# Recommender forward pass: a fill of 224 columns behind every gather, tables split by TensorE, transposes tile by tile with drifting token rows

## Chip, cores, metric

One core of a Trainium2 chip. The metric is the time of one execution in microseconds of that core. The runs of this study fell on several chips of the same kind. They are named by their numbers, because the chip also belong here: on chips 1, 11, 13 and 14 the kernel before takes about 5265 us, on chips 5 and 7 and in the measurement that the prediction is held against about 7120 us. Below, the first are called **quick chips**, the second **slow chips**. Ratios are the mean time of one kernel's fast runs over that of the other's of the same rounds on the same chip, so they are not quite the ratio of the medians quoted beside them.

## The reference

16,384 examples. Each has 32 token ids (table of 50,000 x 300), three lists of 20 ids (tables of 1,000, 5,000 and 10,000 rows of 64) and four single ids.

```python
tok = word_emb[token_idx].mean(axis=1)
e1 = emb_mh1[mh1_idx].mean(axis=1)      # e2, e3 alike
o1 = emb_oh1[oh1_idx]                   # o2, o3, o4 alike
emb = jnp.concatenate([tok, e1, e2, e3, o1, o2, o3, o4], axis=1)     # 748 wide
wide = (wide_mh1[mh1_idx].sum(axis=(1, 2)) + ...)[:, None]           # one number each
h = jax.nn.relu(emb @ W1 + b1)          # 748 -> 1024
h = jax.nn.relu(h @ W2 + b2)            # -> 512
h = jax.nn.relu(h @ W3 + b3)            # -> 256
return jax.nn.sigmoid(h @ Wd + bd + wide)
```

## The kernel before

Examples are worked on in 128 tiles of 128. The token rows come by 32 gathers per tile, 4096 in all, issued by GpSimd and added up by VectorE in pairs:

```python
for q in range(n_groups):                     # 16 pairs per tile
    rows = tokp.tile([P, TOK_GROUP * TOK_D], F32, name="tok_rows")     # 6 buffers
    for r in range(TOK_GROUP):
        j = q * TOK_GROUP + r
        nc.gpsimd.indirect_dma_start(                                  # L224
            out=rows[:, r * TOK_D : (r + 1) * TOK_D], out_offset=None, in_=word,
            in_offset=bass.IndirectOffsetOnAxis(ap=it[:, j : j + 1], axis=0))
    under_way.append((t, q, rows))
    if len(under_way) > TOK_LAG:
        add_up(*under_way.pop(0))             # VectorE, L211 to L215
```

The small tables are not gathered: VectorE makes one-hot rows, TensorE multiplies them into counts, ScalarE evicts the counts and TensorE multiplies them with the tables. A tile has 11 such steps, 1408 in all:

```python
pc = ps_c.tile([P, 2, 2, 512], F32, name="pc")        # one buffer
... nc.tensor.matmul(pc[...], hot[0][half, k, :], hot[1][half, k, :])  # L312, 12 per step
nc.scalar.activation(cnt[...], pc[...], AF.Copy, scale=0.5)            # L319, 1.5 us
... nc.tensor.matmul(pg[:, j, :], by_slice[:, :, h], terms[:, h, :])   # L337, 138 per tile
```

The layers run on blocks of four tiles, in matmuls of 512 columns spread over the steps:

```python
x = xp.tile([P, NK, BLOCK], F32, name="x", tag="even")     # BLOCK = 512
yield from transposed(x, gs)              # four tiles at once, six chunks
yield from layer(h1, w1_sb, b1_sb, x, chunk_k, M1, n)      # matmul L388, eviction on ScalarE
...
sizes = [NSUB] * (tiles // NSUB - 1) + [NSUB - 2, 1, 1]    # last blocks: 2, 1 and 1 tiles
```

Each f32 table is split into three bf16 terms by ScalarE and VectorE at the start (`scalar_tensor_tensor`).

Of the kernel before, what the change touches and what calls it, by code (L numbers as in the profile page):

```python
# [23 lines left out]
TOK_LAG = 3  # L24
BLOCK = 512
HALF = P // 2
N_SMALL = 3 * N_MH + 4
ONEHOT = 6
STEPS = -(-HALF // ONEHOT)
CHUNK_WORK = 1  # L30
TABLE_PACE = 1.2
LAYER_TIME = 10
# [6 lines left out]
G_COLS = TOK_D + 7 * ROW  # L39
# [7 lines left out]
def kernel(  # L47
# [23 lines left out]
    NSUB = BLOCK // P  # L71
# [5 lines left out]
    for f in SMALL:  # L77
# [4 lines left out]
    tokp = ctx.enter_context(tc.tile_pool(name="tok", bufs=2 * TOK_LAG))  # L82
    const = ctx.enter_context(tc.tile_pool(name="const", bufs=1))
    idxp = ctx.enter_context(tc.tile_pool(name="idx", bufs=2))
# [4 lines left out]
    gp = ctx.enter_context(tc.tile_pool(name="g", bufs=NSUB + 1))  # L89
    wp = ctx.enter_context(tc.tile_pool(name="wide", bufs=2 * NSUB))  # L90
    xp = ctx.enter_context(tc.tile_pool(name="x", bufs=1))
# [8 lines left out]
        [(0, 128)],  # L100
        [(128, 256)],
        [(256, 300), (684, 748)],
        [(300, 428)],
        [(428, 556)],
        [(556, 684)],
    ]
# [7 lines left out]
    scale = const.tile([P, NK], F32, name="scale")  # L114
    nc.vector.memset(scale, 1.0)
    nc.vector.memset(scale[:, 0:2], 1.0 / N_TOK)
    nc.vector.memset(scale[0 : TOK_D - 256, 2:3], 1.0 / N_TOK)
    nc.vector.memset(scale[:, 3:4], 1.0 / N_MH)
    nc.vector.memset(scale[0:EMB, 4:5], 1.0 / N_MH)
# [23 lines left out]
    PART = n_h // 6  # L143

    def load_tables(part0, tag):
        raw = xp.tile([P, PART, ROW], F32, name="raw", tag=tag)
        for f in SMALL:
            table, (h0, h1) = tables[f], slices[f]
            full, rest = divmod(table.shape[0], P)
            a, b = max(h0, part0), min(h0 + full, part0 + PART)  # L150
            if a < b:
                nc.sync.dma_start(
                    out=raw[:, a - part0 : b - part0, :],
                    in_=table[(a - h0) * P : (b - h0) * P, :].rearrange("(h p) d -> p h d", p=P),
                )
            if rest and part0 <= h0 + full < part0 + PART:
                nc.vector.memset(raw[:, h0 + full - part0, :], 0.0)
                nc.sync.dma_start(out=raw[0:rest, h0 + full - part0, :], in_=table[full * P :, :])
        return raw

    def convert_tables():


        tags = ("even", "odd")
        raws = [load_tables(k * PART, tags[k]) for k in range(2)]
        yield
        for part in range(n_h // PART):
            rows = raws[part]
            if 1 <= part < n_h // PART - 1:
                raws.append(load_tables((part + 1) * PART, tags[(part + 1) % 2]))  # L170
            for c in range(3):
                term = [
                    terms[:, part * PART : (part + 1) * PART, k * ROW : (k + 1) * ROW]
                    for k in range(3)
                ]
                if c:
                    nc.vector.scalar_tensor_tensor(
                        rows, rows, 2.0 if c == 1 else 1.0, term[c - 1], op0=ALU.mult, op1=ALU.subtract
                    )
                nc.scalar.activation(term[c], rows, AF.Copy, scale=2.0 if c == 0 else 1.0)  # L180
                yield 1
# [20 lines left out]

    n_groups = N_TOK // TOK_GROUP
    under_way = []
    features = {}

    def add_up(t, q, rows):
# [4 lines left out]
        else:  # L212
            nc.vector.tensor_add(tok_sum, tok_sum, a)  # L213
            to = features[t][:, 0:TOK_D] if q == n_groups - 1 else tok_sum
            nc.vector.tensor_add(to, tok_sum, b)  # L215

    def tokens(t, it):


        for q in range(n_groups):  # L220
            rows = tokp.tile([P, TOK_GROUP * TOK_D], F32, name="tok_rows")
            for r in range(TOK_GROUP):
                j = q * TOK_GROUP + r
                nc.gpsimd.indirect_dma_start(  # L224
                    out=rows[:, r * TOK_D : (r + 1) * TOK_D],
                    out_offset=None,
                    in_=word,
                    in_offset=bass.IndirectOffsetOnAxis(ap=it[:, j : j + 1], axis=0),
                )
            under_way.append((t, q, rows))  # L230
            if len(under_way) > TOK_LAG:
                add_up(*under_way.pop(0))
            yield 1

    def last_tokens():
        for group in under_way:
            add_up(*group)

    def load_indices(blk):
# [15 lines left out]
        return it, ix  # L255
# [71 lines left out]
    def small_sums(g, cnt):  # L327
# [3 lines left out]
        for i in (0, 2, 4, 6):  # L331
# [9 lines left out]
            at = TOK_D + i * ROW  # L341
# [9 lines left out]
    def wide_term(g):  # L351
        wide = wp.tile([P, 1], F32, name="wide")
        at = TOK_D + EMB
        nc.vector.tensor_reduce(
            wide,
            g[:, at : at + 6 * ROW].rearrange("p (c d) -> p c d", d=2 * ROW)[:, :, 0:2],
# [3 lines left out]
        nc.vector.tensor_add(wide, wide, g[:, G_COLS - 1 : G_COLS])  # L360
        return wide

    def chunk(g, k):
        if k < 2:
            return g[:, k * P : (k + 1) * P]
        if k == 2:
            return g[:, 2 * P : TOK_D + EMB]
        at = TOK_D + (1 + 2 * (k - 3)) * ROW + 1
        return g[:, at : at + 2 * EMB]

    def transposed(x, gs):

        n = len(gs) * P
        for k in range(NK):
            kk = chunk_k[k]
            pt = ps_h.tile([P, BLOCK], F32, name="pt", tag="ph")
            for s, g in enumerate(gs):
                nc.tensor.transpose(pt[:kk, s * P : (s + 1) * P], chunk(g, k), ident)  # L378
            nc.vector.tensor_scalar(  # L379
                x[:kk, k, 0:n], pt[:kk, 0:n], scale[:kk, k : k + 1], None, ALU.mult  # L380
            )
            yield CHUNK_WORK

    def layer(dst, weights, bias, src, kks, n_out, n):
        for m in range(n_out):
            ph = ps_h.tile([P, BLOCK], F32, name="ph", tag="ph")
            for k, kk in enumerate(kks):
                nc.tensor.matmul(  # L388
                    ph[:, 0:n],
                    weights[:kk, k, m * P : (m + 1) * P],  # L390
                    src[:kk, k, 0:n],
                    start=(k == 0),
                    stop=(k == len(kks) - 1),
                )
                if k < len(kks) - 1:
                    yield 1
            nc.scalar.activation(dst[:, m, 0:n], ph[:, 0:n], AF.Relu, bias=bias[:, m : m + 1])  # L397
            yield 1

    def mlp(b0, gs, wides):  # L400

        n = len(wides) * P
        x = xp.tile([P, NK, BLOCK], F32, name="x", tag="even")
        yield from transposed(x, gs)
        h1 = xp.tile([P, M1, BLOCK], F32, name="h1", tag="odd")
        yield from layer(h1, w1_sb, b1_sb, x, chunk_k, M1, n)
        h2 = xp.tile([P, M2, BLOCK], F32, name="h2", tag="even")
        yield from layer(h2, w2_sb, b2_sb, h1, [P] * M1, M2, n)
        h3 = xp.tile([P, M3 + 1, BLOCK], F32, name="h3", tag="odd")
        yield from layer(h3, w3_sb, b3_sb, h2, [P] * M2, M3, n)  # L410
        po = ps_h.tile([1, BLOCK], F32, name="po", tag="ph")
        for k in range(M3):
            nc.tensor.matmul(  # L413
                po[:, 0:n], wd_sb[:, k : k + 1], h3[:, k, 0:n], start=(k == 0), stop=False
            )
        for s, wide in enumerate(wides):
            nc.tensor.matmul(  # L417
                po[:, s * P : (s + 1) * P], wide, ident, start=False, stop=(s == len(wides) - 1)
            )
        y = h3[0:1, M3, 0:n]  # L420
        nc.scalar.activation(y, po[:, 0:n], AF.Sigmoid, bias=bd_sb)
# [3 lines left out]
    class Paced:  # L425


        def __init__(self, gen):
            self.gen, self.done = gen, 0

        def to(self, size):
            while self.done < size:
                work = next(self.gen, None)
                if work is None:
                    return
                self.done += work
# [27 lines left out]

    tiles = B // P
    mlp_time = (NK * (CHUNK_WORK + M1) + M1 * M2 + M2 * M3 + M3) * LAYER_TIME
    ctx.enter_context(tc.manual_schedule())
    sizes = [NSUB] * (tiles // NSUB - 1) + [NSUB - 2, 1, 1]
    it, ix = load_indices(0)
# [5 lines left out]
    gs, wides, layers, before, b0 = [], [], None, None, 0  # L475
    for t in range(tiles + 1):
        s = t % NSUB
        sums = None
        if before:
            features[t - 1] = g = gp.tile([P, G_COLS], F32, name="g")  # L480
            sums = sums_by_step(small_sums(g, before))
        if t < tiles:
            if s == 0 and t:
                it, sc = next_it, next_sc
            cnt = cp.tile([P, 2, HALF, n_h], FP8, name="cnt", tag="counts")
            toks = Paced(tokens(t, it[:, s, :].bitcast(U32)))
        else:
            last_tokens()
        for i in range(STEPS):
            if t < tiles:  # L490
                hot_now = hot
                if s == 1 and i == 0 and t + NSUB < tiles:
                    next_it, ix = load_indices(t // NSUB + 1)
                if s == 2 and i == 0 and t + NSUB < tiles + 1:
                    next_keys = lookup_keys(ix)
                if i < STEPS - 1:
                    hot = one_hots(sc, s, i + 1)
                elif t + 1 < tiles:
# [66 lines left out]
```

## Time and profile before

| | before |
|---|---|
| timed, three runs | 7126.95 us (7116.23 to 7129.94) |
| profiled execution | span 5269.3 us |
| busy in it: TensorE, VectorE, ScalarE, GpSimd | 97%, 72%, 46%, 74% |
| mean granted TensorE clock in it | 0.989 |

The profile's span and the times differ by 35%. That is the oddity of this case, and the prediction turns on how it is read. A row of the groups gives a line, engine, operation, count, then busy time and mean ns of one, then the engine's idle time just before them and what ended most of it.

### The profile page before, as it was taken

To read this page: it belongs to the slowest core of one execution; us is meant where nothing else is said; L and a number is where in the kernel's file an instruction comes from. 1 tells how busy PE (TensorE), PEld (TensorE's weight loads), DVE (VectorE), ACT (ScalarE), POOL (GpSimd) and SP (SyncE) were. 2 spreads that over 40 slices of the span, in tenths; PEclk is the share of its full clock that TensorE was granted. 3 is DMA by queue.
4 is the path that set the end of the run, shared out by engine and by line. 5 is a ranking of instruction groups with operands and counts; after the bars stand their busy time and mean duration, and the time that the engine had idled before them with its cause. 6 is when DMAs were issued, how large, how long until landed. Compare 5 with 4: busy or idle time off the path is not lost.

```text
span 5269.3 us, 104252 instructions
## 1 busy us (share of the span) xinstructions
PE 5094.7 (97%) x41320; PEld 3164.7 (60%) x41320; DVE 3768.8 (72%) x8014; ACT 2447.1 (46%) x1938; POOL 3897.3 (74%) x4103
## 2 busy tenths in 40 slices
PE   4799999999999999999999999999999999999999
PEld 3565656566565656656655656556566566656658
DVE  8777777777777777777777777777777777777752
ACT  5444444444444444444444444444444444444432
POOL 7777777777777777777777777777777777777762
PEclk8899999999999999999999999999999999999999
DMA  6444444444444444444444444444444444444431
GB/s 190 125 125 124 125 125 126 126 125 124 125 125 125 125 124 125 125 125 126 125 124 125 126 125 126 124 125 125 125 125 125 124 126 125 125 125 125 124 103 34
DMA packets 252890, 652.60 MB, mean 124 GB/s; under 512 B 119009, under 2 KB 119524, under 8 KB 252399
## 3 DMA queue, kind: packets, MB, share of 16 engines
q0 software_dynamic: 196608, 629.41, 43.5%
q1 hardware_dynamic: 55791, 16.53, 1.4%
q8 instruction: 323, 5.29, 0.4%
q14 instruction: 168, 1.38, 0.1%
HBM read 645.59 MB, written 0.07 MB: 123 GB/s over the span
## 4 chain that ended last, share of the span: by engine, by line
PE 37%; DMA 23%; DVE 16%; issue 14%; POOL 10%; ACT 0%; DVEq 0%; SPq 0%; POOLq 0%; ACTq 0%
DMA tok_rows<-in_word_emb_dram,it 22%; PE ph L388 20%; PE pg L337 12%; POOL tok_rows L224 10%; DVE own L215 5%; PE pc L312 4%; DVE own L213 3%; DVE slice L294 3%; DVE row L294 2%; DVE x L379 1%; DVE g L343 1%; PE po L413 1%; DVE own L211 0%; DVE g L215 0%; PE po L417 0%
## 5 line engine op out<-in xcount | busy, mean ns | idle before, releaser
L224 POOL DMA_INDIRECT tok_rows<-in_word_emb_dram,it x4096 | 3896.4, 951 | 1293.4 <-issue 755.5
L319 ACT ACTIVATE cnt<-pc 128x1656 fp8e3<-128x1656 f32 (+1 forms) x1408 | 2121.7, 1507 | 2056.4 <-PE pc L312 2026.0
L337 PE MATMUL pg<-terms,cnt 128*128 128x195 bf16 x17664 | 1849.6, 254 | 87.7 <-DVE g L343 86.3
L337 PEld LDWEIGHTS <-cnt 128*128 128x128 fp8e3 x17664 | 1601.3, 144 | 234.6 <-issue 81.1
L388 PE MATMUL ph<-x,w_sb 128*128 128x512 f32 (+5 forms) x3264 | 1474.1, 581 | 4.2 <-DVE x L379 3.5
L215 DVE TENSOR_TENSOR own<-own,tok_rows 128x300 f32<-128x300 f32 x1792 | 857.7, 479 | 680.6 <-DMA tok_rows<-in_word_emb_dram,it 647.3
L388 PE MATMUL ph<-h,w_sb 128*128 128x512 f32 (+2 forms) x2720 | 1211.0, 573 | 0.0
L213 DVE TENSOR_TENSOR own<-own,tok_rows 128x300 f32<-128x300 f32 x1920 | 918.8, 479 | 387.6 <-DMA tok_rows<-in_word_emb_dram,it 335.8
L312 PEld LDWEIGHTS <-row 64*128 64x128 bf16 x16384 | 501.7, 95 | 1041.3 <-DVE own L215 246.1
L294 DVE TENSOR_TENSOR row<-own,sc 128x768 bf16<-128x768 bf16 (+1 forms) x1408 | 762.4, 541 | 162.8 <-PE pc L312 89.5
L312 PE MATMUL pc<-slice,row 64*128 64x138 bf16 x16384 | 758.4, 224 | 70.6 <-DVE slice L294 36.7
L388 PEld LDWEIGHTS ph<-x,w_sb 128*128 128x128 f32 (+1 forms) x3264 | 564.3, 194 | 414.6 <-issue 401.9
L294 DVE TENSOR_TENSOR slice<-own,sc 128x828 bf16<-128x828 bf16 (+1 forms) x1408 | 797.9, 567 | 0.0
L388 PEld LDWEIGHTS ph<-h,w_sb 128*128 128x128 f32 x2720 | 463.3, 192 | 317.9 <-issue 316.0
L397 ACT ACTIVATE h<-ph,b_sb 128x512 f32<-128x512 f32 (+2 forms) x476 | 316.3, 665 | 683.2 <-PE ph L388 678.2
L343 DVE TENSOR_REDUCE g<-pg 128x130 f32<-128x390 f32 (+1 forms) x512 | 259.2, 506 | 151.1 <-PE pg L337 150.8
L379 DVE TENSOR_SCALAR x<-pt,scale 128x512 f32<-128x512 f32 (+4 forms) x204 | 137.0, 712 | 3.7 <-PE pt L378 2.9
L378 PE MATMUL pt<-ident,g 128*128 128x128 f32 (+1 forms) x768 | 104.1, 275 | 3.0 <-DVE x L379 2.5
L211 DVE TENSOR_TENSOR own<-tok_rows 128x300 f32<-128x300 f32 x128 | 61.4, 480 | 49.5 <-DMA tok_rows<-in_word_emb_dram,it 47.3
L378 PEld LDWEIGHTS pt<-ident,g 128*128 128x128 f32 (+1 forms) x768 | 85.5, 141 | 7.7 <-DVE x L379 6.7
L215 DVE TENSOR_TENSOR g<-own,tok_rows 128x300 f32<-128x300 f32 x128 | 60.2, 471 | 22.3 <-DMA tok_rows<-in_word_emb_dram,it 18.3
L413 PE MATMUL po<-h,wd_sb 128*1 128x512 f32 (+2 forms) x136 | 60.9, 566 | 0.3
(34 smaller groups left out, 290.1 us busy)
## 6 DMA issues: line engine op xcount, KB each, us to landing
tok_rows<-in_word_emb_dram,it POOLq DMA_INDIRECT x4096
ix<-in_idx_dram SPq DMA_DIRECT2D x128, 32.0 KB
w_sb<-in_W_dram SPq DMA_DIRECT2D x6, 512.0 KB
raw<-in_mh_dram SPq DMA_DIRECT2D x3, 747.5 KB
it<-in_idx_dram SPq DMA_DIRECT2D x32, 64.0 KB
w_sb<-in_W_dram SPq DMA_DIRECT2D x1, 2048.0 KB
raw<-in_mh_dram SPq DMA_DIRECT2D x1, 617.5 KB
out_dram<-h SPq DMA_DIRECT2D x31, 2.0 KB
```

Of the source, the lines that this page charges most:

```text
L213: nc.vector.tensor_add(tok_sum, tok_sum, a)
L215: nc.vector.tensor_add(to, tok_sum, b)
L224: nc.gpsimd.indirect_dma_start(out=rows[:, r * TOK_D : (r + 1) * TOK_D], out_offset=None, in_=word, in_offset=bass.IndirectOffsetOnAxis(ap ...
L294: nc.vector.tensor_tensor(one[:, 0:rows, :].rearrange("p i (n d) -> p i n d", d=2), iota[:, 0:n].rearrange("p (n d) -> p n d", d=2).unsque ...
L312: nc.tensor.matmul(pc[:, f, k // n, at : at + n_h], hot[0][half, k, :], hot[1][half, k, :], start=True, stop=True,)
L319: nc.scalar.activation(cnt[:, :, b : b + rows, :].rearrange("l f (g k) h -> l f g (k h)", g=2), pc[:, :, :, 0 : n * n_h], AF.Copy, scale=0 ...
L337: nc.tensor.matmul(pg[:, j, :], by_slice[:, :, h], terms[:, h, :], start=(h == h0), stop=(h == h1 - 1))
L343: nc.vector.tensor_reduce(g[:, at : at + n * ROW].rearrange("p (f d) -> p f d", f=n), pg[:, 0:n, :].rearrange("p f (c d) -> p f d c", c=3) ...
L378: nc.tensor.transpose(pt[:kk, s * P : (s + 1) * P], chunk(g, k), ident)
L379: nc.vector.tensor_scalar(x[:kk, k, 0:n], pt[:kk, 0:n], scale[:kk, k : k + 1], None, ALU.mult)
L388: nc.tensor.matmul(ph[:, 0:n], weights[:kk, k, m * P : (m + 1) * P], src[:kk, k, 0:n], start=(k == 0), stop=(k == len(kks) - 1),)
L397: nc.scalar.activation(dst[:, m, 0:n], ph[:, 0:n], AF.Relu, bias=bias[:, m : m + 1])
```

## The change

The intent, as the code shows it: space the gathers by a fill, let the token rows run evenly over the whole program instead of tile by tile, take work off VectorE at the start, and avoid the squeeze at the end. Layers work on two tiles (256 columns) instead of four.

```diff
+PAUSE = 224
+TOK_BUFS = 8
+WAKE = 16
+LAYER_TILES = 2
...
-    tokp = ctx.enter_context(tc.tile_pool(name="tok", bufs=2 * TOK_LAG))
+    tokp = ctx.enter_context(tc.tile_pool(name="tok", bufs=TOK_BUFS))
...
                     nc.gpsimd.indirect_dma_start(
                         ...
                     )
+                    nc.gpsimd.memset(pause, 0.0)        # 128 x 224 f32, read by nobody
...
-                if c:
-                    nc.vector.scalar_tensor_tensor(
-                        rows, rows, 2.0 if c == 1 else 1.0, term[c - 1], op0=ALU.mult, op1=ALU.subtract
-                    )
-                nc.scalar.activation(term[c], rows, AF.Copy, scale=2.0 if c == 0 else 1.0)
+            nc.tensor.matmul(left, twice, rows(p), start=True, stop=False)
+            for k in range(c):
+                nc.tensor.matmul(left, minus, term(p, k), start=False, stop=(k == c - 1))
+            nc.scalar.activation(term(p, c), left, AF.Copy)
...
-            pt = ps_h.tile([P, BLOCK], F32, name="pt", tag="ph")
-            for s, g in enumerate(gs):
-                nc.tensor.transpose(pt[:kk, s * P : (s + 1) * P], chunk(g, k), ident)
+            pt = ps_h.tile([P, 4, P], F32, name="pt", tag="ph")       # one tile's small sums
+            nc.tensor.transpose(pt[:, 3, :], g[:, 0:P], ident)
+            ...                                                        # its token sums apart
...
-            ph = ps_h.tile([P, BLOCK], F32, name="ph", tag="ph")
+            ph = ps_h.tile([P, N], F32, name="ph", tag="ph")          # N = 256
...
-                toks.to(n_groups * (i + 1) / STEPS)
+        toks.to(n_all * (step + 1) / n_steps)      # n_steps = tiles * STEPS + WAKE
...
-    sizes = [NSUB] * (tiles // NSUB - 1) + [NSUB - 2, 1, 1]
+    sizes = [LAYER_TILES] * (tiles // LAYER_TILES - 1) + [1] * LAYER_TILES
```

## The prediction

> **What bounds the kernel now.** I read the times first. The three timed runs lie at 7116 to 7130 us, but the profiled execution of the same kernel took 5271 us on its own clock. So the profile shows a run 1856 us quicker than the ones to be predicted. The first question is which engine the quick run hangs on, the second what could stretch by 35% when the profiler is off.
>
> I then read the page's busy shares and slices, because they show at once whether one engine is level from end to end.
>
> ```profile
> PE   4799999999999999999999999999999999999999
> ...
> POOL 7777777777777777777777777777777777777762
> PEclk8899999999999999999999999999999999999999
> ```
>
> TensorE looks full from the third slice on and its clock is granted. GpSimd is level at 7 from the first slice to the 38th, and even where TensorE has only 4 tenths of work. An engine that waited for TensorE would not be so level there. So I asked the timeline of GpSimd, at the start and in the middle (columns: start, duration, instruction, idle before it).
>
> ```profile
> 9.54 0.94 POOL L224 DMA_INDIRECT tok_rows<-in_word_emb_dram,it  x1 [0.30 <-issue]
> 10.79 0.95 POOL L224 DMA_INDIRECT tok_rows<-in_word_emb_dram,it  x1 [0.30 <-issue]
> 12.05 0.95 POOL L224 DMA_INDIRECT tok_rows<-in_word_emb_dram,it  x1 [0.30 <-issue]
> ...
> 2009.66 0.96 POOL L224 DMA_INDIRECT tok_rows<-in_word_emb_dram,it  x1 [0.30 <-issue]
> 2010.93 0.95 POOL L224 DMA_INDIRECT tok_rows<-in_word_emb_dram,it  x1 [0.31 <-issue]
> 2012.18 0.95 POOL L224 DMA_INDIRECT tok_rows<-in_word_emb_dram,it  x1 [0.30 <-DVE own L213]
> ```
>
> Gathers start 1.25 us apart from beginning to end: 0.95 us of work and a 0.30 us hole which nothing else fills. Over the whole trace 4038 of 4095 intervals are 1.24 to 1.27 us. The first gather starts at 3.1 us and the last at 5190.4, and 4096 x 1.2525 = 5130 us of that is this beat. The rest is 58 us of longer intervals, 43 of them in the last 270 us, where the layers of the last full block are squeezed into two tiles and TensorE sets the pace. So **the profiled run is bound by the issue of gathers**. The groups say the same: GpSimd's idle time is mostly "issue", and VectorE's adds wait for rows from DMA.
>
> ```profile
> L224 POOL DMA_INDIRECT tok_rows<-in_word_emb_dram,it x4096 | 3896.4, 951 | 1293.4 <-issue 755.5
> ...
> L215 DVE TENSOR_TENSOR own<-own,tok_rows 128x300 f32<-128x300 f32 x1792 | 857.7, 479 | 680.6 <-DMA tok_rows<-in_word_emb_dram,it 647.3
> ```
>
> TensorE is second. By start-to-start times in the timeline (ten 512-column matmuls in 4.48 us, the last counting 0.606: 0.43 each; fifteen table matmuls in 1.52 us: 0.090; twelve count matmuls in 0.54 us: 0.029) its work is 5456 x 0.43 + 17664 x 0.090 + 16384 x 0.029 + about 150 for the small ones = 4560 us, 87% of the span and not 97%.
>
> The timed runs exceed the profiled one by 1856 / 4096 = 0.453 us per gather, so if gathers bind there too they come every 1.70 us. I take this as the likeliest reading: with nothing in the hole, unprofiled gathers queue up closer on GpSimd and each takes longer. This is an inference; no line of the profile shows an unprofiled gather.
>
> [...] here spacing (1.25) and span (0.95) differ by 0.30 us, so I use spacing. [...] at 21.03 us VectorE's 1.72 us table subtraction began and the gather at 22.07 took 1.50 us instead of 0.95. [...] the granted clock here is 0.989 on average[...].
>
> **The change part by part.**
>
> Fill. It adds 4096 fills of 128x224 f32 on GpSimd, each behind its gather. The kernel has a fill of 128x128 f32 at 205 ns (the row below) and four of one column at 98 to 118 ns: 0.76 ns per column, so 224 columns are about 108 + 223 x 0.76 = 278 ns. That is nearly the 0.30 us hole. Gather and fill are 0.95 + 0.28 = 1.23 us, against a beat of 1.25. I choose that the fill takes the hole's place and gives the unprofiled run the spacing of the profiled one, 1.25 us, perhaps up to 0.05 more. Nobody would have settled on an odd 224 if it only added time.
>
> ```profile
> masks.py:197 POOL MEMSET ident<- 128x128 f32 x1 | 0.2, 205 | 0.3 <-POOLq L550 0.3
> ```
>
> Tables. Twelve VectorE subtractions of 1.71 us (20 us) go, with the 11 us by which they held gathers up in the first 100 us. TensorE gets 20 pieces of 455 columns, each with two f32 and three bf16 products, about 42 us, in slices where it is a third idle. Nothing on the path.
>
> Layers of 256 columns in place of 512. Twice as many matmuls of half the width: the six 256-column ones at 5204.75 took 1.46 us with a last one of 0.38, so 0.216 each, and 63 blocks x 176 x 0.216 + 2 x 176 x 0.112 = 2434 us against about 2400 before. The weight loads (192 ns) still hide under 216. TensorE's sum becomes about 4640 us, still under the gathers.
>
> Transposes tile by tile. Seven instead of six per tile (0.107 us each, +14 us of TensorE). Evictions on VectorE by its eviction rows (349 ns for 128 columns, 480 for 256, 743 for 512): about 0.61 + 0.35 + 0.35 + 0.48 + 0.35 = 2.1 us per tile, 274 us against 140. VectorE goes from 3769 to about 3900 us, off the path.
>
> Drift. Token groups are spread evenly over all steps and 16 more, in place of tile by tile, and the last two blocks are one tile each, with no double-sized block squeezed in before them. This should recover most of the 43 us at the end. The tail shrinks from 77 us (5190 to 5269) to about 30: landing and last adds 4, transposes 2, and the layers of one tile, which the chain shows as 20 us:
>
> ```profile
> 5245.92 19.97 PE ph L388 x176
> ```
>
> Sum: 3 + 4096 x 1.2525 + 5 of blocked gathers in the body + 30 = 5168 us; with 0.015 us more per gather for dispatch of the fill, 62 us, about 5230.
>
> **The rivals.**
> 1. The fill adds to the 1.25 us beat instead of filling its hole: 4096 x 1.53 + 35 = 6300 us. For it: the hole could be the gather's own cost before the next instruction. Against it: the tuned size.
> 2. The slow spacing of 1.70 stays and the fill comes on top: 4096 x 1.98 + 30 = 8140 us, slower. For it: GpSimd is in order and has no spare time in such a run. Against it: a fill there would have no reason.
> 3. The timed runs are slower because TensorE's clock is lower; then the fill is hidden, TensorE's work is +80 us in 4640, and the time stays near 7100. For it: TensorE is at 87% in the profile, so a clock of about 0.65 would give 7127. Against it: the clock granted in the profile, and a busy TensorE that nothing starves.
> 4. TensorE becomes the bound once gathers are quick: its 4640 us plus waits for evictions of 256-column blocks, perhaps 5300 to 5400. This would only shade the gain.
>
> **Range and chances.** The cure near 1.25 to 1.33 us per gather (5090 to 5500) has some 0.67, the additive cure (5500 to 6400) 0.13, a weak one 0.02. Rival 3 gets 0.07, rival 2 0.11. The lower end, 5090, allows a spacing of 1.235; the upper end takes in rival 1.
>
> **What would show it.** In the profile of the changed kernel: a MEMSET of about 280 ns between gathers, gathers still 1.25 us apart (1.53 would be rival 1), a tail after the last gather of about 30 us, no SCALAR_TENSOR_TENSOR, layer matmuls of 256 columns 0.216 apart, GpSimd in 9s. Above all, the timed runs must come within a few per cent of the profiled one: the gap of 1856 us must close. If the gap stays while the profile looks the same, the gather explanation is wrong; if timed runs rise above 7.5 ms, rival 2 was right.

## The result

| | before | after |
|---|---|---|
| timed | 7122.07 us (7116.23 to 7129.94, 4 runs) | 7216.63 us (7203.92 to 7228.62, 4 runs) |
| ratio | | 1.0132, 95% interval 1.0110 to 1.0153 |
| span of the profile | 5269.3 us | 7211.6 us |
| mean granted TensorE clock | 0.989 | 0.899 |

The change made no difference of 2%. The forecast of 5230 us missed by 38%. The gap between timed and profiled run is gone, but the other way round: the profile rose to the times. So the profile of before must come from another condition than its times, while the profile of after shows the condition in which both kernels were timed. **The two profiles cannot be compared as if only the kernel differed.** For such comparisons the experiments below supply pairs (e12 and after are one kernel in the two conditions; e10 and e16 another).

The slices of after, which answer those of before in the prediction:

```profile
PE   6877878878788787788888888888887888887878
...
POOL 7777767777777667777777777777777777676775
PEclk8898898999999888899889989989999899888889
```

TensorE is no longer full in any stretch, its clock dips everywhere, and GpSimd is at 7 although it now has the fill as well. Nothing is level at 9: this run is bound by no engine's work. The groups of after show waiting instead:

```profile
L259 POOL DMA_INDIRECT tok_rows<-in_word_emb_dram,it x4096 | 3905.1, 953 | 2038.9 <-DVE own L246 1281.7
L352 ACT ACTIVATE cnt<-pc 128x1656 fp8e3<-128x1656 f32 (+1 forms) x1408 | 2123.0, 1508 | 3106.7 <-remote 1469.3
...
L327 DVE TENSOR_TENSOR row<-own,sc 128x768 bf16<-128x768 bf16 (+1 forms) x1408 | 762.3, 541 | 1508.1 <-remote 1082.1
...
L265 POOL MEMSET pause<- 128x224 f32 x4096 | 1231.9, 301 | 2.0
...
L246 DVE TENSOR_TENSOR own<-own,tok_rows 128x300 f32<-128x300 f32 x1792 | 856.9, 478 | 61.8
```

A gather still takes 953 ns of GpSimd, as in the profile of before (951), so gathers are not 1.7 us each. The adds of L246, which waited for token rows before, now hardly wait (62 us): rows lie ready. GpSimd waits 1282 us for VectorE to free buffers, and VectorE and ScalarE wait 1082 and 1469 us for "remote" before the groups shown. On one core there is no other core; the word means that the profile has no record of the signal that ended the wait. In the chain that ended last the same hole stands second:

```profile
PE 49%; another core or an unknown queue 21%; DVE 16%; issue 8%; ACT 6%; POOL 0%; DVEq 0%; DMA 0%; ACTq 0%; POOLq 0%
```

What such a wait is, the timeline of after shows (start, duration, instruction, idle before it and its releaser):

```profile
3008.93 0.54 PE L345 MATMUL pc<-slice,row 64*128 64x138 bf16 x12
...
3013.09 0.56 DVE L327 TENSOR_TENSOR row<-own,sc 128x768 bf16<-128x768 bf16 x1 [3.41 <-PE ph L447]
3013.09 1.55 ACT L352 ACTIVATE cnt<-pc 128x1656 fp8e3<-128x1656 f32 x1 [4.45 <-PE ph L447]
...
3014.69 0.55 PE L345 MATMUL pc<-slice,row 64*128 64x138 bf16 x12 [2.01 <-DVE own L242]
```

The count matmuls end at 3009.47. ScalarE needs nothing else to evict them, and VectorE nothing else to overwrite the one-hot rows; yet both start together at 3013.09, 3.62 us later, and TensorE then stands idle for 2.01 us. The same place in a trace of the same kernel on a quick chip (e12):

```profile
3004.70 0.54 PE L345 MATMUL pc<-slice,row 64*128 64x138 bf16 x12
...
3005.29 1.55 ACT L352 ACTIVATE cnt<-pc 128x1656 fp8e3<-128x1656 f32 x1 [2.13 <-PE pc L345]
```

Here the eviction starts 0.05 us after the last count (3005.24). **In the slow condition TensorE's completion signals arrive late.** (Ends of matmuls are modelled in the profile, so it can't tell a late signal from a late completion.) I measured it over whole traces: for each matmul that raises a semaphore, the time from its recorded end (with 60 ns of tolerance) to the next recorded update of that semaphore.

```
ns from a TensorE matmul's end to the semaphore's update: median, 90%, mean
quick chip:  before (e1)         19     20     30
             after (e12)         14     19     60
slow chip:   after, first trace 297   3274   1065
             after (e5)         421   2797   1003
             after without fill (e8)  110   4236   1305
```

The records are thinned in the slow condition as well: of one semaphore that counts landings of gathers, 8164 updates are recorded in e12 and 2322 in the first trace of after, the same kernel. A lost record makes the measured delay too long, so these means are rough.

A second measure needs no such records: how long after the last count matmul the counts eviction starts, where ScalarE was already free. It is 42 to 43 ns, median and mean, in every quick run; in the slow condition the mean is 1.30 us (after), 1.33 (e5), 1.26 (e8), 1.72 (e6) and 1.94 (e16), with 90% points of 3.7 to 6.6 us. The way back is not late: where TensorE waits for that eviction, its next count matmul starts 51 to 54 ns (mean) after the eviction's end in all five of these traces. So TensorE's signals are late and ScalarE's are not; that GpSimd's waits for VectorE follow from the former is an inference.

### The profile page after: what moved, and what is told of

The parts are those of the page before. It is cut to its first block, busy times and chain, and to the rows that moved or that the text cites. A ratio compares the mean times of both kernels' runs of the same rounds, so it can differ in the third digit from the quotient of the medians.

```text
span 7211.6 us, 120614 instructions
## 1 busy us (share of the span) xinstructions
PE 5813.3 (81%) x46912; PEld 4623.2 (64%) x46912; DVE 3896.3 (54%) x8503; ACT 2586.2 (36%) x2445; POOL 5129.5 (71%) x8199
## 3 DMA queue, kind: packets, MB, share of 16 engines
q0 software_dynamic: 196608, 629.41, 31.8%
## 4 chain that ended last, share of the span: by engine, by line
PE 49%; another core or an unknown queue 21%; DVE 16%; issue 8%; ACT 6%; POOL 0%; DVEq 0%; DMA 0%; ACTq 0%; POOLq 0%
PE ph L447 22%; PE pg L370 15%; PE pc L345 8%; DVE own L242 5%; ACT cnt L352 5%; DVE slice L327 4%; DVE own L246 4%; PE po L472 1%; DVE row L327 1%; ACT h L456 1%; PE pt L415 1%; PE pt L431 1%; PE pt L432 1%; PE left L196 1%
## 5 line engine op out<-in xcount | busy, mean ns | idle before, releaser
L352 ACT ACTIVATE cnt<-pc 128x1656 fp8e3<-128x1656 f32 (+1 forms) x1408 | 2123.0, 1508 | 3106.7 <-remote 1469.3
L370 PE MATMUL pg<-terms,cnt 128*128 128x195 bf16 x17664 | 2113.3, 271 | 213.2 <-issue 173.8
L370 PEld LDWEIGHTS <-cnt 128*128 128x128 fp8e3 x17664 | 1770.7, 146 | 460.9 <-issue 338.9
L447 PE MATMUL ph<-h,w_sb 128*128 128x256 f32 (+1 forms) x5200 | 1346.0, 403 | 49.3 <-issue 29.8
L265 POOL MEMSET pause<- 128x224 f32 x4096 | 1231.9, 301 | 2.0
L447 PE MATMUL ph<-x_small,w_sb 128*128 128x256 f32 (+3 forms) x4160 | 1154.2, 406 | 67.7 <-issue 26.0
L447 PEld LDWEIGHTS ph<-h,w_sb 128*128 128x128 f32 x5200 | 1001.2, 205 | 204.8 <-issue 65.9
L456 ACT ACTIVATE h<-ph,b_sb 128x256 f32<-128x256 f32 (+1 forms) x910 | 426.9, 469 | 1438.5 <-PE ph L447 624.3
L447 PEld LDWEIGHTS ph<-x_small,w_sb 128*128 128x128 f32 (+1 forms) x4160 | 807.2, 208 | 195.5 <-issue 68.3
L246 DVE TENSOR_TENSOR own<-own,tok_rows 128x300 f32<-128x300 f32 x1792 | 856.9, 478 | 61.8
L447 PE MATMUL ph<-x_tok,w_sb 128*128 128x256 f32 (+1 forms) x2080 | 617.8, 404 | 12.3 <-issue 11.6
L447 PEld LDWEIGHTS ph<-x_tok,w_sb 128*128 128x128 f32 x2080 | 404.0, 207 | 76.1 <-issue 27.4
```

Source lines behind the costliest of these rows:

```text
L246: nc.vector.tensor_add(to, tok_sum, b)
L265: nc.gpsimd.memset(pause, 0.0)
L352: nc.scalar.activation(cnt[:, :, b : b + rows, :].rearrange("l f (g k) h -> l f g (k h)", g=2), pc[:, :, :, 0 : n * n_h], AF.Copy, scale=0 ...
L447: nc.tensor.matmul(ph[:, 0:n], weights[: src.shape[0], k, m * P : (m + 1) * P], src, start=(k == 0), stop=(k == len(srcs) - 1),)
L456: nc.scalar.activation(dst[:, m, 0:n], ph[:, 0:n], AF.Relu, bias=bias[:, m : m + 1])
```

## The experiments

Four questions: is the slow condition a matter of the profiler or the chip; what does the fill cost where signals are prompt; what do the fill and the rest do where signals are late; and what makes signals late. Every kernel passed the comparison with the reference, even those that are wrong on purpose, as its tolerance is wide.

### Quick chip 1: before again, and the parts of the change apart

e1 is before, unchanged. e2 is after without the fill. e3 is before with the fill. e4 is after, fill kept, with one gather per pair (wrong on purpose).

```diff
 # e2                                           # e3 is the same line added to before
-                    nc.gpsimd.memset(pause, 0.0)
 # e4
-                for r in range(TOK_GROUP):
+                for r in range(1):             # 2048 gathers; add_up takes the first half twice
```

> The kernel before, unchanged, to get its profile in the state in which it is timed. My theory on record (slow gathers when nothing stands between them): time 7120 us, and its profile, if it falls in that state, shows gathers of more than 0.95 us, start to start about 1.70 us without a wait between. Rival, from the profile of the changed kernel (late signals: TensorE's completions reach VectorE and ScalarE some us after the matmuls' recorded ends): 7120 us, gathers still 0.95 us and 1.25 us apart in bursts, with waits for VectorE of about 1.3 to 1.9 ms in total, and ScalarE's evictions of counts waiting 2 to 3 ms. If the profile again shows about 5270 us while the timed runs show 7120, the profile itself changes the state.

> The changed kernel without the fill. Slow gathers: without the fill it is slower than with it, or the same at 7100 to 7300 us with gathers 1.70 us apart. Late signals: the fill does not matter much as GpSimd waits 1.3 ms for VectorE anyway; 7000 to 7300 us, waits of ScalarE and VectorE for TensorE as before, GpSimd waiting some 1.2 ms more for VectorE.

> The kernel before with the fill of 224 columns behind each gather and nothing else. Slow gathers (cure): 5300 to 5900 us. Fill added to the beat: 1.42 us per gather by the changed kernel's profile, so 5850 us or more. Late signals: the fill changes little, 7000 to 7300 us.

> The changed kernel with one gather per pair instead of two (2048 instead of 4096; both adds use the same rows, so the result is wrong on purpose; all work of TensorE, VectorE and ScalarE stays). Late signals caused by the traffic of the gathers: TensorE's signals come in time, and the time falls to TensorE's own sum, 4650 to 5200 us. Late signals with another cause (TensorE's own stream or its clock): stays at 6800 to 7200 us. Slow gathers: 2048 x 1.7 = 3500 us is under TensorE's sum, so 4650 to 5200 us too, but with TensorE's signals in time in both kernels.

| chip 1, before 5261.44 us | median us | ratio to before |
|---|---|---|
| e1 before | 5261.23 | 1.0000 |
| e2 after, no fill | 5184.40 | 0.9855 (0.9839 to 0.9872) |
| e3 before + fill | 5958.82 | 1.1327 (1.1308 to 1.1346) |
| e4 after, half the gathers | 5184.96 | 0.9856 (0.9839 to 0.9872) |

Timed runs of before take 5261 us here, and its profiled run 5273. So there is no gap between timed and profiled runs on one chip; there are two conditions. What the fill does on GpSimd is seen in after's own timeline on chip 14 (e12 below):

```profile
2000.28 0.95 POOL L259 DMA_INDIRECT tok_rows<-in_word_emb_dram,it  x1 [0.17 <-issue]
2001.24 0.30 POOL L265 MEMSET pause<- 128x224 f32 x1
2001.70 0.95 POOL L259 DMA_INDIRECT tok_rows<-in_word_emb_dram,it  x1 [0.16 <-issue]
```

The fill starts 0.01 us after the gather, so it does take the 0.30 us hole, but a hole of 0.17 us opens behind it: the beat is 1.42 us and not 1.25. 4096 x 0.17 = 696 us, and e3 is 698 us longer than e1.

e2 and e4 agree within 1 us although e4, which keeps the fill, has half the gathers. So gathers do not bind after without its fill; TensorE does. The busy line of e2:

```profile
PE 5108.7 (99%) x46912; PEld 4172.3 (81%) x46912; DVE 3892.5 (75%) x8503; ACT 2600.8 (50%) x2445; POOL 3890.6 (75%) x4103
```

### Slow chip 7: the same parts again

e5 is after, unchanged; e8 is after without the fill (edit of e2). e6 is before with a fill of 32 columns. e7 is before with one gather per pair, the edit of e4, wrong on purpose.

```diff
 # e6
+    pause = const.tile([P, 32], F32, name="pause")
...
+                nc.gpsimd.memset(pause, 0.0)
```

> The changed kernel, unchanged, beside the kernel before on one chip. If this chip is one where the kernel before takes 5261 us: the fill costs 0.165 us per gather (1.42 us between gathers in the trace of the changed kernel against 1.25), so 3 + 4096 x 1.418 + 30 = about 5840 us, 11% slower than before, TensorE's signals within 20 ns of the recorded ends. If the chip is one where the kernel before takes 7120 us: 7216 us as measured first, signals late by up to several us. If it takes 7200 us on a chip where before takes 5261 us, the late signals belong to the changed kernel and not to the chip.

> The kernel before with a fill of 32 columns behind each gather (224 columns gave 5959 us against 5261). If the fill costs what it has beyond the hole that it fills (hole of 0.30 us behind a gather, 0.17 us behind a fill, fill of 32 columns about 0.14 us): 0.95 + 0.14 + 0.17 = 1.26 us between gathers, 5261 to 5320 us. If every further instruction on GpSimd costs a fixed amount whatever its length: 5700 to 5960 us.

> The kernel before with one gather per pair instead of two (wrong on purpose; adds and all TensorE work stay). If the issue of gathers alone bounds the kernel before, as I predicted: TensorE's sum of 4560 us shows, so 4650 to 4900 us. If TensorE with its switches between kinds of matmul (about 0.1 us each, three a step, 1408 steps) bounds it as nearly: 5100 to 5250 us.

> The changed kernel without the fill, a second time, to have it beside the changed kernel on one chip whatever state that chip is in. Chip where before takes 5261 us: 5184 us. Chip where before takes 7120 us: late signals make up the time and the fill only uses waiting time of GpSimd, 7050 to 7300 us; or the fill is a cure for that state, then over 7400 us without it.

| chip 7, before 7119.59 us | median us | ratio to before | clock |
|---|---|---|---|
| e5 after | 6918.93 | 0.9727 (0.9708 to 0.9745) | 0.915 |
| e6 before + fill of 32 columns | 7128.14 | 1.0014 (0.9990 to 1.0039) | 0.901 |
| e7 before, half the gathers | 5155.55 | 0.7245 (0.7232 to 0.7257) | 0.996 |
| e8 after, no fill | 7549.57 | 1.0612 (1.0594 to 1.0630) | 0.878 |

Three things follow. **The change is two effects of opposite sign here.** Without the fill it costs 6.1%; the fill takes 631 us (8.4%) off that. In the first measurement the two came out at +1.3%, here at -2.7%; that difference of 4% between two slow conditions I cannot explain, and the sum should be read as "about nothing". Why the rest of the change costs 6.1% here is not shown; after has 3343 matmuls that raise a semaphore where before has 2680, so more late signals to wait for would fit. A fill of 32 columns (e6, expected only for a quick chip) moves nothing; before with 224 columns was not run on a slow chip.

Second, halving the gathers removes the slow condition: 5155 us, granted clock 0.996, on a chip where before takes 7120 us. Third, chip 7 is not slower at everything: e7 takes about what the halved kernel with tiny transfers takes on a quick chip (5149, e9 below). A trace of the condition is left even then: its counts evictions start 66 ns after the last count in the mean, not 42.

GpSimd's row shows where the fill's 631 us come from. With the fill (e5), then without (e8):

```profile
L259 POOL DMA_INDIRECT tok_rows<-in_word_emb_dram,it x4096 | 3914.8, 956 | 1720.5 <-DVE own L246 1003.3
```

```profile
L259 POOL DMA_INDIRECT tok_rows<-in_word_emb_dram,it x4096 | 3876.7, 946 | 3626.1 <-DVE own L246 2322.7
```

And before itself in the slow condition, with the small fill of e6 (before alone was timed there, but not profiled):

```profile
L225 POOL DMA_INDIRECT tok_rows<-in_word_emb_dram,it x4096 | 3909.6, 954 | 2564.7 <-DVE own L216 1547.9
```

In all three a gather takes 0.95 us. The fill of after adds 1237 us to GpSimd, but GpSimd had 3626 us of idle time, 2323 of it waiting for VectorE; the fill uses time that was waited away. The rest of the kernel gains: from e8 to e5 TensorE is busy for 269 us less and idle for 369 us less, and it stood at half clock in 1172 instead of 1844 us.

The clock goes with these waits. The traces list the granted clock as 1.0 or 0.5, in stretches that are whole multiples of 3.41 us (487 of 488 in the first trace of after, 49 of 50 in that of before; the last of each is cut short by the end). In the first trace of after TensorE was busy for 0.30 (median) of the 3.4 us before each of 242 falls, against 0.81 over the span. It seldom waited in one piece: 18% of the falls had one hole of 3.4 us in the 10 us before. Quick chips agree in direction (e2 busy 99%, clock 0.999; e11 busy 84%, clock 0.94). So the low clock comes where TensorE waits, and I take it as a consequence; the chip can grant nearly the full clock, as e7 shows (0.996).

How the fill gains its 631 us stays open. My reading was that wider spacing makes signals less late; the traces are mixed on it. Counts evictions start as late in the mean with the fill as without (1.33 and 1.26 us; 90% points 3.7 and 4.8), layer evictions less late (0.27 and 0.49), and no run changed spacing alone in the slow condition.

### What makes signals late: updates, bytes or gathers

Each gather brings 16 completion updates (65,351 are recorded in e1 on the eight semaphores that count landings of gathers), bytes, and an instruction of GpSimd with its packets. A tiny transfer of e9 brings 16 as well (e13's trace has 31,339 more on eight other semaphores than e1's). Adding updates to the halved kernel (e9, e13, e15) and halving the bytes of the whole one (e10, e14, e16), both wrong on purpose, take these apart, but only on a slow chip; it took three calls to meet one.

```diff
 # e9, e13, e15: before with one gather per pair, and behind each
+            mark = tinyp.tile([16, 1], F32, name="mark")
+            nc.sync.dma_start(out=mark, in_=word[0:16, 0:1])
 # e10, e14, e16: rows of 600 bytes; word_halves is the table as 100,000 rows of 150
-                    out=rows[:, r * TOK_D : (r + 1) * TOK_D],
+                    out=rows[:, r * 150 : (r + 1) * 150],
-                    in_=word,
+                    in_=word_halves,
```

> The kernel before with half the gathers (as e7, 5155 us on the chip where before takes 7120) plus 2048 transfers of 16 x 4 bytes from SyncE's queue, one for each gather left out: almost no bytes, but as many completions on semaphores (16 each) as in the kernel before. On a chip where before takes 7120 us: if the number of semaphore updates (or of their records) is what makes signals late, the slow state comes back, 6500 to 7300 us. If it is the gathers' bytes or GpSimd's own work, 5150 to 5300 us. On a chip where before takes 5261 us: 5150 to 5300 us, which tells nothing.

> The kernel before with one gather per pair and 2048 transfers of 64 bytes by SyncE, wrong on purpose. On a slow chip: if the number of completion updates makes signals late, 6500 to 7300 us; if bytes or GpSimd's gathers do, 5150 to 5300. On a quick chip 5150 either way, as in its first run.

> Halved gathers with 2048 transfers of 64 bytes by SyncE, wrong on purpose. On a slow chip: 6500 to 7300 us if the number of completion updates makes signals late, 5150 to 5300 if bytes or GpSimd's gathers do. On a quick chip 5150 either way.

> The kernel before with all 4096 gathers, each of 600 bytes a row instead of 1200 (wrong on purpose; adds unchanged). On a chip where before takes 7120 us: if bytes cause the late signals, 5150 to 5300 us; if the number of gathers or of semaphore updates does, 6800 to 7200 us. On a chip where before takes 5261 us: 5261 us, as GpSimd's beat of 1.25 us stays.

> The kernel before with 4096 gathers of 600 bytes per row in place of 1200, wrong on purpose. On a slow chip: if bytes make signals late, 5150 to 5500 us; if the number of gathers or of their updates does, 6800 to 7200. On a quick chip 5270 either way, as in its first run.

> 4096 gathers of 600 bytes per row, wrong on purpose. On a slow chip: 5150 to 5500 us if bytes make signals late, 6800 to 7200 if the number of gathers or of their updates does. On a quick chip 5265 either way.

| | chip | before us | median us | ratio |
|---|---|---|---|---|
| e9, e13 half the gathers + tiny transfers | 11, 14 | 5267.90, 5263.86 | 5149.17, 5150.10 | 0.9773, 0.9784 |
| **e15** the same | **5, slow** | 7121.81 | **5159.62** | 0.7247 (0.7234 to 0.7259) |
| e10, e14 half the bytes | 11, 14 | 5267.90, 5263.86 | 5272.00, 5264.59 | 1.0008, 1.0000 |
| **e16** the same | **5, slow** | 7121.81 | **7172.75** | 1.0048 (1.0001 to 1.0095) |

On chip 5 adding the updates to the halved kernel does not bring the slow condition back, and halving the bytes does not remove it. The counts eviction of e15 and of e16:

```profile
L322 ACT ACTIVATE cnt<-pc 128x1656 fp8e3<-128x1656 f32 (+1 forms) x1408 | 2121.6, 1507 | 1987.7 <-PE pc L315 1799.4
```

```profile
L320 ACT ACTIVATE cnt<-pc 128x1656 fp8e3<-128x1656 f32 (+1 forms) x1408 | 2122.0, 1507 | 4026.6 <-remote 2463.1
```

With 2048 gathers and the updates of 4096, ScalarE waits as on a quick chip, for TensorE. With 4096 gathers of half the bytes it waits twice as long, and for signals without a record. So what makes signals late comes with the **number of gathers** (or their rate, which these runs don't separate from it), at full or half bytes, and is not the mere number of completion updates. Whether it is GpSimd's instruction or the 48 packets that each gather makes (196,608 in all, in e16 as in before) stays open, and so does why only some chips show it. A kernel with 64 rows per gather was meant to tell packets from instructions; it did not build, and no other was run.

Whether the recording of signals has a part in making them late was not shown. Late signals and lost records come together (2322 records against 8164 above). Every run of the experiments lists a granted clock, so none is without some recording, and whether the slow condition exists without any is not known. Against such a part, e15 makes about as many updates as before (79,222 recorded in e13, the same kernel on a quick chip, 80,763 in e1), loses a quarter of the records on its slow chip (58,814 left), and takes 5160 us with a mean delay of 273 ns, against 1385 in e16. Updates and their records in that number are thus not enough to make signals as late.

### What a fill costs where signals are prompt

e11 is after with `PAUSE = 400`, e12 after unchanged. e17 and e18 repeat e11, in the hope of a slow chip; both fell on quick ones (13 and 1).

```diff
-PAUSE = 224
+PAUSE = 400        # e11, e17, e18
```

> The changed kernel with a fill of 400 columns instead of 224: about 0.45 us, so a beat of 0.95 + 0.45 + 0.17 = 1.57 us and a floor of 4096 x 1.57 + 30 = 6460 us. On a chip where before takes 7120 us: if spacing the gathers is what the fill is good for, it comes near that floor, 6450 to 6900 us, where 224 columns gave 6919 and none 7550. If the fill works only by a small pause, it is slower than with 224 columns, over 7000 us. On a chip where before takes 5261 us: 6460 us.

> The changed kernel as it is. On a chip where the kernel before takes about 5265 us: the fill costs 0.30 us plus a hole of 0.17 us behind each gather of 0.95 us, so 1.42 us per gather, 4096 x 1.42 + 25 = about 5840 us, 11% slower than before (additive beat of 1.53 would give 6300, a fill that hides in the hole 5180 to 5230). On a chip where the kernel before takes about 7120: 6900 to 7220, within 3% of before.

> The changed kernel with a fill of 400 columns in place of 224: gathers at least 1.57 us apart on GpSimd, the same gathers, bytes and completion updates. On a slow chip: if the spacing of the gathers makes signals late, near the 6489 us of the quick chip, 6450 to 6700; if their number alone does, with waits adding to the longer beat, 6900 to 7400. On a quick chip 6490 again.

> The changed kernel with a fill of 400 columns, gathers at least 1.57 us apart on GpSimd. On a slow chip: if spacing gathers that far avoids late signals, near the 6482 to 6489 us of quick chips, up to 6700; if each gather causes about 1.7 us of work elsewhere that backs up, no better than the 6919 us of the fill of 224, so 6850 to 7000; if waits add to the longer beat, 7000 to 7400. On a quick chip 6485 again.

| | chip | before us | median us | ratio |
|---|---|---|---|---|
| e12 after | 14 | 5263.86 | 5869.73 | 1.1152 (1.1134 to 1.1171) |
| e11 after, 400 columns | 11 | 5267.90 | 6489.42 | 1.2316 (1.2295 to 1.2336) |
| e17, e18 the same | 13, 1 | 5264.57, 5273.41 | 6482.48, 6493.73 | 1.2313, 1.2314 |

The cost model holds: 4096 x (0.95 + 0.30 + 0.17) + 25 = 5841 for e12, measured 5870. For 400 columns the fill takes 449 ns (1840.4 / 4096), and 4096 x (0.95 + 0.45 + 0.17) + 25 = 6456, measured 6482 to 6494. On a quick chip the change is **11.5% slower**, and all of it is the fill: without it the change is 1.5% faster (e2, within the 2% that counts as the same). The groups of e12, to be held against those of after's first trace, are the same kernel in the other condition:

```profile
L259 POOL DMA_INDIRECT tok_rows<-in_word_emb_dram,it x4096 | 3902.4, 953 | 710.7 <-issue 583.1
L352 ACT ACTIVATE cnt<-pc 128x1656 fp8e3<-128x1656 f32 (+1 forms) x1408 | 2123.2, 1508 | 1818.2 <-PE pc L345 1747.4
...
L246 DVE TENSOR_TENSOR own<-own,tok_rows 128x300 f32<-128x300 f32 x1792 | 857.4, 478 | 963.8 <-DMA tok_rows<-in_word_emb_dram,it 939.3
```

Every duration is the same (953, 1508, 478 ns). Only the waits differ: GpSimd idles for 711 instead of 2039 us, ScalarE for 1818 instead of 3107 and for a named releaser, and the adds wait for rows (964 instead of 62 us), which is what a run bound by gathers looks like. Of the 1345 us between the two spans (7211.6 and 5867.0), TensorE's busy time has 535 (5813.3 at a mean granted clock of 0.899 against 5278.2 at 0.970) and its idle time 810. A lower clock lengthens the busy time: in after's first trace a layer matmul of 256 columns over 128 rows takes 383 ns in the mean where the clock is 1.0 and 644 where it is 0.5.

What stays open: whether a longer fill would help more on a slow chip. None of these versions beats before on both kinds of chips: after without its fill is best on quick ones (-1.5%) and worst on slow ones (+6.1%).

## Why the prediction was wrong, by its own steps

- **"If gathers bind there too they come every 1.70 us": this step failed, and the forecast with it.** I took the 1856 us between times and profile for a lengthening of each gather that the profiler prevents. Gathers take 0.95 us in both conditions (e1 952 ns; on slow chips e6 954, e16 948). What is longer is the waiting for TensorE's late signals, on some chips: counts evictions start 1.3 to 1.9 us after the last count in the mean, against 42 ns, and GpSimd then waits for buffers (1282 us in after). I called the step an inference without a line behind it, and then gave it 0.67.
- **"The fill takes the hole's place": wrong by 0.17 us per gather.** Its own duration was sized almost right (278 predicted, 301 measured), and it does start in the hole; the hole behind it was not foreseen. Rival 1 expected the whole fill on top, 1.53 us; the beat is 1.42.
- **TensorE's sum of 4640 us was too small.** Without its fill the changed kernel is bound by TensorE at 5184 us, busy for 5109 (e2, e4). The durations of single matmuls were right; what is missing is the switch between kinds of them. One step of e2 (the lines below), from one group of counts (3004.38) to the next (3008.07), takes 3.69 us, and its 12 x 0.029 + 15 x 0.090 + 8 x 0.216 give 3.43. That is 0.26 us for the switches, some 370 us over 1408 steps, an estimate that accounts for most but not all of the 544. The lines show where: into and out of the counts, which use 64 rows of the array; from table to layer matmuls nothing is lost. Over all of e2 a count starts 311 ns after a layer matmul (layers: 216 apart) and a table matmul 155 ns after a count (counts: 29 apart). So before was bound by gathers (5261), as I said, but with TensorE 2% behind (e7, 5155) and not 13%.

```profile
3004.38 0.54 PE L344 MATMUL pc<-slice,row 64*128 64x138 bf16 x12
3004.86 1.52 PE L369 MATMUL pg<-terms,cnt 128*128 128x195 bf16 x15
3006.22 1.49 PE L446 MATMUL ph<-x_small,w_sb 128*128 128x256 f32 x6
3007.54 0.59 PE L446 MATMUL ph<-x_tok,w_sb 128*128 128x256 f32 x2
3008.07 0.42 PE L344 MATMUL pc<-slice,row 64*128 64x138 bf16 x8
```

- **Sum without the fill, 5168 us:** e2 gave 5184. Close, but TensorE set that time and not the gathers (e4), whose own floor lay just below; that the two nearly met is luck.
- **The end and the tables were right.** In after the last gather starts at 7169.79 and the run ends at 7211.6, 42 us later where I had 30 (28 us on a quick chip, e12); the layers of the last tile take 20 us of it, as predicted (the line below is from the chain of after that ended last). Before had 79 us of tail by the traces (the prediction read 77); from e1 to e2 it falls from 79 to 34, which is 45 of the 88 us between the two traces (77 between the medians).

```profile
7187.90 20.14 PE ph L447 x176
```

- **Rival 3** (a lower TensorE clock, about 7100, "same") came nearest in the time. Half of its mechanism was there: the clock granted was 0.899, and the fill is hidden in part. But the clock looks like a consequence: chips 5 and 7 grant 0.996 once the gathers are halved. Rival 2 (8140) did not come: GpSimd had idle time that the fill could use (3626 us without it, e8).
- **"the gather at 22.07 took 1.50 us instead of 0.95"** (beside a table subtraction of VectorE): true of the table subtractions, but not of every VectorE instruction with two SBUF inputs. The gathers beside the twelve subtractions took 1.5 us in the mean; the 2257 that ran mostly beside the token adds, which also have two SBUF inputs, took 0.95. It touched 11 us of the sum, so nothing hung on it.
- **"Nobody would have settled on an odd 224 if it only added time"** was right for slow chips, where it saves 8.4%, and wrong for quick ones, where it adds 13%.

The sentence that should have counted for more was my own: if the gap stays while the profile looks the same, the gather explanation is wrong. A profile 35% quicker than the times of the same kernel describes another condition. I should have given much of the probability to "the profile does not show what bounds the timed runs", and with it a range that reaches past 7100 us.

## What to carry to other kernels

Where times and profile of one kernel differ by far more than their own scatter, first measure both on the same chip; a forecast from the profile speaks only for the condition in which it was taken. A fill or another delay that was tuned by trial belongs to that condition: here the same 224 columns save 8% on one chip and cost 13% on another. Before something is put into a hole of the engine that sets the pace, ask what hole will stand behind it; and when durations are equal and only waits grow, look at how late the waiters start after the end of what they wait for.
